# Attention over 1,426 keys: the last 32 keys' scores once per image, the last pair's sum on TensorE, third expert layers every other step

## The chip, the cores and the metric

One core of one Trainium2 chip runs the whole network in one launch. The metric is the device time of that launch in microseconds. Before the change three runs took 3327.84 to 3328.48 us, median 3328.4. The profiled execution has a span of 3332.1 us; all shares below are of that span.

## The reference, cut to what matters

The input is 8 images of 256 channels and 32 x 32 places, float32. Layer 0 is an attention with pooled keys, layer 1 an attention over 1024 tokens and then eight experts. The change touches the softmax attention of layer 0 and the end of the experts:

```python
# layer 0, for each image: 8 heads of 32 channels, 1024 queries, N = 1024 + 256 + 121 + 25 = 1426 keys
attn = softmax(einsum('bhqd,bhkd->bhqk', q_g, k) * SCALE, axis=-1)
out_att = einsum('bhqk,bhkd->bhqd', attn, v)
# layer 1, experts: three layers per expert e, weighted by a gate per place
h = relu(bn(einsum('bfd,edh->bfeh', x, W1)))
h = relu(bn(einsum('bfeh,ehk->bfek', h, W2)))
y = einsum('bfeh,ehd->bfed', h, Wo) + bo
out = einsum('bfed,fe->bfd', y, w)
```

## The kernel before, in words

**Recording layer.** Nearly every instruction goes through one helper (`call` in `Flow.Engine`, line 669), so the profile shows line 669 for all of them and names have to be told by their tiles. `Flow` also plans: it keeps a modelled clock for each engine (`cost`, `now`), and background work is written as generators ("threads"). Between two pieces of the main loop `f.step(pace)` runs threads whose inputs are ready by the model, with a credit of TensorE time given by `PACE` (threads of high rank) and `PACE1` (those of rank 5 and above). `f.finish(cond)` runs threads until a condition holds. All this happens when the program is built. On the chip the order on each engine is then fixed, and only semaphores remain.

**The attention stage, 0 to about 2,000 us.** A unit is one image `b`, one half `c` of the heads (four heads) and one half of the queries (512), so there are 4 units per image and 32 in all. `KEY_CHUNKS` (line 43) cuts the 1,426 keys into 12 chunks: eleven of 128 and a last one of 18. The main loop has a step for each unit and chunk, 384 steps:

- `scores`: four matmuls, one for each head, each 32 rows of the array, write the tile `sc` [128 keys, 4 heads, 512 queries]. `sc` is four PSUM banks, and there is only one of it. ScalarE then writes exp of it into a tile `pt` (1 MB; there are six buffers).
- `values` of the step before: four matmuls, one for each head, each 32 columns of the array, add up in `pv` over the 12 chunks.
- After each odd chunk, `add` issues a DMA from GpSimd's queue that adds this `pt` to the one before it in place (`accum_op`), so a pair becomes one tile.
- `sums`, a thread of rank 0 for each unit: VectorE adds pair after pair to the first (five pairs, two instructions each), then TensorE multiplies the total with ones (four matmuls of 32 columns) and so sums over the 128 keys. ScalarE copies the result into `rec`, and `normalise` divides.

As background run the pooled maps, convolutions and layernorms of the next image's keys and values, and layer 1's attention for the image before.

**The expert stage, about 2,000 to 3,332 us.** There are 128 items (16 tiles of 512 places, eight experts). `first7` and `second` compute layers one and two by seven block products each (tile `bank`), which VectorE combines (`sums`). `second(i, True)` writes its result to DRAM, and `fetch` reads it back. `weigh` multiplies it by the gate on VectorE and makes the combinations `t` for the third layer, on VectorE or GpSimd. `third` does seven products into `y`. Third layers can't start before the gate is known, which needs the mean over all images; by then the second layers are 24 or so ahead. The loop at the end of `experts` (from line 2339) lets the third layers catch up: while `many` is true, it does two of them in each iteration. For the first of the two, GpSimd makes the combinations and, for the second, VectorE.

Of the kernel before, what the change touches and what calls it, by code (L numbers as in the profile page):

```python
# [16 lines left out]
P = 128  # L17
C = 256
HW = 1024
HEADS = 8  # L20
DH = 32
# [7 lines left out]
FILLER = 5  # L29
PACE = 4.0  # L30
PACE1 = 2.0
CAP = (1.5, 1.5)
# [9 lines left out]
LIMIT = 1e12  # L42
KEY_CHUNKS = [(i * P, min(P, NK - i * P)) for i in range(NKC)]
KEY_SLICES = [(0, 512), (512, 512), (1024, 402)]
# [98 lines left out]
def layer0_general(tc, kit, nb, x, t1, consts, consts8, vecs, q_t, kv_t, proj_t, gqk_t):  # L143
    nc = tc.nc
    T = kit.tile
    with ExitStack() as ctx:
# [189 lines left out]
        def transpose_values(b):  # L336
            acc = vs.pop(b)
            for i in range(0, NKC, 2):
                ps = T(psum, [P, 512], "sm")
                part = KEY_CHUNKS[i : i + 2]  # L340
                for u, (k0, w) in enumerate(part):
                    for c in range(2):
                        o = u * C + c * P
                        nc.tensor.transpose(ps[:w, o : o + P], acc[:, c, k0 : k0 + w], ident)
                whole = [part] if part[-1][1] == P else [part[:1], part[1:]]
                u = 0
                for group in whole:
                    w, g = group[0][1], len(group)
                    src = ps[:w, u * C : (u + g) * C].rearrange("p (a j d) -> p a j d", j=2, d=DH)
                    dst = vext[:w, i + u : i + u + g].rearrange("p u a s d -> p (u a) s d")  # L350
                    nc.vector.tensor_copy(dst[:, :, 0, :], src[:, :, 0, :])
                    nc.scalar.copy(dst[:, :, 2, :], src[:, :, 1, :])
                    u += g

        def global_token(b):
# [21 lines left out]
            ps = T(psum, [P, 512], "sm")  # L377
            for kc, (k0, w) in enumerate(KEY_CHUNKS):
                nc.tensor.transpose(ps[:w, kc * 8 : kc * 8 + 8], pg[:, k0 : k0 + w], ident[:HEADS, :HEADS])
            pt = T(work, [P, NKC * 8], "gpt")  # L380
            last, lw = (NKC - 1) * 8, KEY_CHUNKS[-1][1]
            nc.vector.tensor_copy(pt[:, :last], ps[:, :last])
# [3 lines left out]
            ps = T(psum, [P, 512], "sm")  # L386
            for kc, (k0, w) in enumerate(KEY_CHUNKS):
                nc.tensor.matmul(
                    ps[:HEADS, :C],
                    lhsT=pt[:w, kc * 8 : kc * 8 + 8],  # L390
                    rhs=vext[:w, kc, :, 0::2, :],
                    start=kc == 0,
                    stop=kc == NKC - 1,
                )
# [144 lines left out]
        def attend(n, background, steps):  # L539
# [4 lines left out]
            for half in range(2):  # L544
# [13 lines left out]

                for kc, (k0, w) in enumerate(KEY_CHUNKS):
                    t = T(psum, [P, 2, 512], "sc")  # L560
# [95 lines left out]
class Flow:  # L656
# [54 lines left out]
    def cost(self, engine, op, out, ins):  # L711
# [9 lines left out]
        if engine == "PE":  # L721
            if op == "transpose":
                return 0.13
            c = max(0.2, 0.00169 * n)
            return c if self.tiling(ins) is None else c / 4
        psum = any(i.space == PSUM for i in ins)
# [153 lines left out]

def attention(tc, kit, f, outer, ended, nb, consts, x, t1, t2, hn, bounds, vecs, q_t, kv_t, proj_t, gqk_t, wqk, wqkv, vecs1, w1_d, w1c, gate_d, wrc, vecs2, bnvec):

# [5 lines left out]
    with ExitStack() as ctx:  # L888
# [160 lines left out]

        ks, qs, vts = {}, {}, {}  # L1050
        made = [0]
        turn = [-1]
# [199 lines left out]
        def by_tokens(accs, dst, k0):  # L1252
# [4 lines left out]
            for i in range(0, 4, 2):  # L1257
                span = slice(chunks[i][0], sum(chunks[i + 1]))
                yield pe(*(acc[:, span] for acc in accs), tag="sm")
                ps = small()  # L1260
                for u, (o0, w) in enumerate(chunks[i : i + 2]):
                    for c in range(2):
                        o = u * C + c * P
                        f.pe.transpose(ps[:w, o : o + P], accs[c][:, o0 : o0 + w], ident)
                w = chunks[i + 1][1]
                if w == P:
                    f.act.activation(dst[:, i : i + 2, :], ps.rearrange("p (u c) -> p u c", u=2), AF.Copy)
                else:
                    f.act.activation(dst[:, i, :], ps[:, :C], AF.Copy)
                    f.act.activation(dst[:w, i + 1, :], ps[:w, C:], AF.Copy)  # L1270
            yield ve(dst)
# [155 lines left out]
        def key_tokens(b, g):  # L1427
# [7 lines left out]
            for c in range(2):  # L1435
# [5 lines left out]
                ps = small()  # L1441
                for u, (_, tw) in enumerate(KEY_CHUNKS[4 * g : 4 * g + 4]):
                    f.pe.transpose(ps[:, u * P : u * P + tw], kt[:tw, u, c * P : (c + 1) * P], ident[:tw, :tw])
                f.act.activation(ks[b, c][:, s0 : s0 + w], ps[:, :w], AF.Copy)
# [18 lines left out]
        def scores(b, c, sl, kc):  # L1463
# [7 lines left out]
            return pt  # L1471

        def values(b, c, kc, pt, pv):
            w = KEY_CHUNKS[kc][1]
# [17 lines left out]
        def sums(n, pairs):  # L1492

            for i in range(1, NKC // 2):
                yield until(lambda: len(pairs) > i)
                for j in range(0, 4, 2):
                    s = pairs[0][:, j : j + 2, :]
                    yield ve(s, pairs[i])
                    f.ve.tensor_tensor(s, s, pairs[i][:, j : j + 2, :], ALU.add)
            yield until(lambda: normalised[0] == n)  # L1500
            yield pe(pairs[0], tag="sm")
            total = small()
            for j in range(4):
                f.pe.matmul(
                    total[DH * j : DH * j + DH, :], lhsT=kit.ones[:, :DH], rhs=pairs[0][:, j, :], start=True, stop=True
                )
            rec = T(work, [P, 512], "rec")
# [303 lines left out]
        f.spawn(layer1(), 6)  # L1811
        steps = [(b, c, half, kc) for b in range(nb) for c in range(2) for half in range(2) for kc in range(NKC)]

        pts = {}
        for i in range(len(steps) + 1):
            if i < len(steps):
                b, c, half, kc = steps[i]
                sl = slice(half * 512, half * 512 + 512)
# [8 lines left out]
                if b == 0 and kc == 0:  # L1827
                    f.finish(lambda: (c, half) in asked)
                pts[i] = scores(b, c, sl, kc)
                f.step()  # L1830
            if i:
                b1, c1, half1, kc1 = steps[i - 1]
                if kc1 == 0:
                    pv = T(psum, [P, 512], "pv")
                    pairs = []
                    sl1 = slice(half1 * 512, half1 * 512 + 512)
                    f.spawn(unit(b1, c1, sl1, i // NKC, pairs), 0)
                f.finish(lambda: kc1 // 4 in vts[b1])
                values(b1, c1, kc1, pts[i - 1], pv)
                if kc1 % 2:  # L1840
                    add(kc1, pts.pop(i - 1), pts[i - 2])
                    pairs.append(pts.pop(i - 2))
                if kc1 == NKC - 1:
# [145 lines left out]
def experts(tc, kit, nb, t2, hn, h2d, w1c, w2_d, wo_d, bnvec, bo_d, gate_d, wrc, consts8, gtd, out, f, outer, ended, early):  # L1989
# [12 lines left out]
    with ExitStack() as ctx:  # L2002
# [336 lines left out]
        while n3 < total:  # L2339
            many = n2 > n3 + 2  # L2340
            if n2 < n1 - 1 or n1 == total and n2 < total:
                second(n2, many)
                n2 += 1
                if many:
                    weighed(f.pool)
                    thirds()
            weighed(f.ve if many else f.pool)
            if n1 < total:
# [6 lines left out]
def tile_conv_attn_hybrid(  # L2355
# [45 lines left out]
    with ExitStack() as early:  # L2401
# [5 lines left out]
        attention(  # L2407
            tc, kit, f, (l1, shared), ended, nb,
            consts, x, t1, t2, hn, bounds, vecs0, q_t, kv_t, proj_t, gqk_t, wqk, wqkv, vecs1, w1_d, w1c, gate_d, wrc, vecs2, bnvec,
# [124 lines left out]
```

## Time and profile before

| engine | busy, us | share | what it does in the attention step |
|---|---|---|---|
| TensorE (PE) | 3137.4 | 94% | scores, values, ones-products, background |
| its weight loads (PEld) | 1912.8 | 57% | overlap with the matmuls |
| VectorE (DVE) | 2472.4 | 74% | pair sums, convolutions, normalisation |
| ScalarE (ACT) | 1734.4 | 52% | exp, evacuation of PSUM |
| GpSimd (POOL) | 1227.3 | 37% | issues the accumulating DMAs; layer combinations in the experts |

A matmul in float32 stands as two records, so the counts of TensorE records are about twice those of instructions. Groups of the attention step that matter for the change:

| group | records | mean of one, us |
|---|---|---|
| exp, `pt<-sc` | 384 | 1.875 |
| pair sums on VectorE, `pt<-pt,pt` | 320 | 1.254 |
| scores, `sc<-q,kn` | 3072 | 0.650, four at a time |
| values, `pv<-pt,vt` | 3072 | 0.620, four at a time |
| accumulating DMA of 1024 KB, `pt<-pt` | 160 | 7.4 from issue to landing |
| the same of 144 KB (18 keys) | 32 | 4.5 from issue to landing |

The page gives busy time, then what made the engine wait. Busy time of one engine lies beside that of others. Work taken away from an engine counts only where another one waited for it. A wait is written as "who <- for whom: us in total, times, longest".

### The profile page before, as it was taken

The page shows a single profiled execution, that of the slowest core. Times are in us where ns is not written, and L with a number is a line of the kernel's source. Part 1 is how long each engine was busy: PE and PEld are TensorE (multiplying, and loading weights), DVE is VectorE, ACT ScalarE, POOL GpSimd, SP SyncE. Part 2 cuts the span into 40 slices and gives each one's busy share as a digit, 9 for nine tenths or more (in the row PEclk, how much of TensorE's full clock was granted, in tenths as well). Part 3 has the DMA queues.
Part 4 walks back from the last instruction along what each step waited for, and adds up shares of the span by engine and source line. Part 5 has one row for each costly group of instructions (what it writes and reads, how often), then busy time and mean ns, then how long its engine had stood idle before and what let it go on. Part 6 is the DMA issues. An engine that isn't in the chain of part 4 may idle for free.

```text
span 3332.1 us, 42942 instructions
## 1 busy us (share of the span) xinstructions
PE 3137.4 (94%) x15970; PEld 1912.8 (57%) x15970; DVE 2472.4 (74%) x4069; ACT 1734.4 (52%) x2328; POOL 1227.3 (37%) x1300
## 2 busy tenths in 40 slices
PE   8687899999999999899899999999999999999997
PEld 4332244344344344344345346777888888888886
DVE  5687788786887886886884555446998787787776
ACT  4476676666576566576566543333233444444442
POOL 2211413213213214213211112006666776777775
PEclk9798999999999999999999999999999999999999
DMA  2357656656646646656556656124442010000000
GB/s 74 82 121 158 131 106 146 133 101 154 133 100 157 135 104 147 135 120 123 121 125 133 133 119 237 70 88 159 158 146 102 20 45 26 20 20 32 20 13 21
DMA packets 106666, 347.10 MB, mean 104 GB/s; under 512 B 13056, under 2 KB 38408, under 8 KB 83216
## 3 DMA queue, kind: packets, MB, share of 16 engines
q0 software_dynamic: 28608, 179.85, 28.1%
q1 hardware_dynamic: 74480, 162.45, 14.1%
q8 instruction: 128, 2.10, 0.3%
q10 hardware_dynamic: 3360, 1.97, 0.2%
q14 instruction: 90, 0.74, 0.1%
HBM read 105.11 MB, written 73.97 MB: 54 GB/s over the span
## 4 chain that ended last, share of the span: by engine, by line
PE 57%; DVE 5%; issue 3%; ACT 3%; POOL 3%; DMA 2%; SPq 0%; DVEq 0%; POOLq 0%; ACTq 0%
PE bank L669 18%; PE sm L669 13%; PE y L669 8%; PE sc L669 6%; PE sx L669 6%; PE pv L669 5%; DVE h L669 2%; ACT pt L669 2%; POOL tm L669 1%; DVE u L669 1%; DMA pt<-pt 1%; ACT h L669 1%; POOL t L669 1%; DVE t L669 1%; DVE c L669 1%
## 5 line engine op out<-in xcount | busy, mean ns | idle before, releaser
L669 ACT ACTIVATE pt<-sc 128x2048 f32<-128x2048 f32 (+1 forms) x384 | 719.9, 1875 | 326.5 <-PE sc L669 272.7
L669 DVE SCALAR_TENSOR_TENSOR acc<-p,vec,acc 128x225 f32<-128x225 f32 (+7 forms) x928 | 526.6, 574 | 29.3 <-ACT acc L669 4.8
L669 PE MATMUL sc<-q,kn 32*128 32x512 f32 (+1 forms) x3072 | 445.6, 650 | 94.7 <-ACT pt L669 92.9
L669 DVE TENSOR_TENSOR pt<-pt,pt 128x1024 f32<-128x1024 f32 x320 | 387.4, 1254 | 144.3 <-DMA pt<-pt 135.3
L669 POOL DMA_DIRECT2D pt<-pt x192 | 174.0, 907 | 780.1 <-ACT pt L669 615.7
L669 PE MATMUL pv<-pt,vt 128*32 128x512 f32 (+1 forms) x3072 | 420.6, 620 | 0.0
L669 ACT ACTIVATE p1c<-bank 128x256 f32<-128x256 f32 x228 | 87.2, 383 | 576.4 <-PE bank L669 576.1
L669 ACT ACTIVATE h<-h,bnvec 128x512 f32<-128x512 f32 x456 | 345.0, 805 | 50.7 <-DVE h L669 43.7
L669 POOL TENSOR_TENSOR rstd<-rstd,mhalf 128x4 f32<-128x4 f32 (+2 forms) x88 | 107.0, 1216 | 673.8 <-DVE rstd L669 635.0
L669 DVE TENSOR_TENSOR h<-p1c,bank 128x512 f32<-128x512 f32 x228 | 155.2, 681 | 194.7 <-PE bank L669 191.2
L669 PEld LDWEIGHTS sc<-q,kn 32*128 32x128 f32 (+1 forms) x3072 | 116.1, 178 | 285.8 <-ACT pt L669 184.9
L669 POOL TENSOR_TENSOR tm<-h,tm 128x256 f32<-128x256 f32 x206 | 247.6, 1202 | 16.1
L669 DVE TENSOR_TENSOR h<-u,bank 128x256 f32<-128x256 f32 x456 | 232.1, 550 | 7.9
L669 PEld LDWEIGHTS pv<-pt,vt 128*32 128x32 f32 (+1 forms) x3072 | 60.7, 108 | 301.7 <-issue 290.3
L669 POOL TENSOR_TENSOR tm<-h 128x512 f32<-128x512 f32 x103 | 133.9, 1300 | 245.2 <-ACT h L669 241.2
L669 DVE TENSOR_TENSOR h<-h,gate 128x1024 f32<-128x1024 f32 x128 | 209.1, 1642 | 2.5 <-DMA h<-h 2.1
L669 PE MATMUL bank<-h,w2e 128*128 128x256 f32 (+1 forms) x612 | 198.8, 453 | 4.1 <-DVE h L669 4.1
L669 PE MATMUL y<-t,s3e 128*128 128x256 f32 x768 | 188.0, 381 | 10.6 <-POOL t L669 10.3
L669 POOL TENSOR_TENSOR t<-h,t 128x256 f32<-128x256 f32 x210 | 177.4, 845 | 16.5
L669 PE MATMUL bank<-t,s1e 128*128 128x256 f32 x750 | 182.3, 379 | 0.0
L669 PE MATMUL sm<-y,t 128*128 128x256 f32 x752 | 180.6, 385 | 0.0
L669 DVE TENSOR_TENSOR u<-h,bank 128x512 f32<-128x512 f32 x228 | 156.7, 687 | 24.0
(316 smaller groups left out, 5604.3 us busy)
## 6 DMA issues: line engine op xcount, KB each, us to landing
pt<-pt POOLq DMA_DIRECT2D x160, 1024.0 KB, 7.4
h<-h SPq DMA_DIRECT2D x90, 512.0 KB, 3.2
xi<-in_x_dram SPq DMA_DIRECT2D x16, 512.0 KB, 6.7
t<-t SPq DMA_DIRECT2D x8, 1024.0 KB, 9.7
res<-t SPq DMA_DIRECT2D x32, 256.0 KB, 3.9
t<-res SPq DMA_DIRECT2D x32, 256.0 KB, 5.4
hn<-res SPq DMA_DIRECT2D x32, 256.0 KB, 3.0
hn<-hn SPq DMA_DIRECT2D x16, 512.0 KB, 4.2
```

The source lines that it names most:

```text
L669: ins = fn(*args, **kwargs)
```

## The change

**The last 32 keys.** `KEY_CHUNKS` now cuts ten chunks of 128, one of 114 and one of 32 (`LAST`). The scores of the last chunk are computed once per image, for all four units: `last_scores` places unit `n` on the score tile's partitions 32n to 32n + 31, by 16 matmuls of 32 x 32, and one exp serves all four. The part of unit 0 is used in place. Those of units 1 to 3 are written to small DRAM tiles (`lasts`), and `fetch_last` reads each back to partitions 0 to 31 of a `pt` tile, two steps before its unit ends. An image has 12 + 3 x 11 = 45 steps instead of 48. In units 1 to 3 the values of chunks 10 and 11 follow each other in one step.

**The last pair.** `sums` leaves the last pair (chunks 10 and 11) out of VectorE's additions. It gets four ones-products of its own, which accumulate onto those of the first tile. The tile of the last pair is so kept until then.

**Pace.** The credits per step are raised from 4.0 and 2.0 to 4.3 and 2.15, since the same background has to fit in fewer steps.

**Third layers.** In the loop of the experts the additional third layer comes only with every other second layer, with its combinations on VectorE; the regular one has them on GpSimd. The catching up takes about twice as many iterations.

```diff
-PACE = 4.0
-PACE1 = 2.0
+PACE = 4.3
+PACE1 = 2.15
...
+LAST = 32
+KEY_CHUNKS = [(i * P, P) for i in range(NKC - 2)]
+KEY_CHUNKS += [((NKC - 2) * P, NK - LAST - (NKC - 2) * P), (NK - LAST, LAST)]
...
+            if self.key(out).startswith("sc") and ins[0].shape[-1] == LAST:
+                return c / 16
...
+        def last_scores(b):
+            k0 = KEY_CHUNKS[-1][0]
+            t = T(psum, [P, 4, 512], "sc")
+            for n in range(4):
+                c, half = divmod(n, 2)
+                for j in range(4):
+                    r = slice(DH * j, DH * j + DH)
+                    f.pe.matmul(
+                        t[LAST * n : LAST * n + LAST, j, :],
+                        lhsT=ks[b, c][r, k0:],
+                        rhs=qs[b, c][r, half * 512 : half * 512 + 512],
+                        start=True,
+                        stop=True,
+                    )
+            pt = T(work, [P, 4, 512], "pt", bufs=6)
+            f.act.activation(pt, t, AF.Exp, scale=SCALE0)
+            for n in range(1, 4):
+                f.sp.dma_start(lasts[n - 1], pt[LAST * n : LAST * n + LAST])
+            return pt
+
+        def fetch_last(n):
+            pt = T(work, [P, 4, 512], "pt", bufs=6)
+            f.sp.dma_start(pt[:LAST], lasts[n - 1])
+            return pt
...
-            for i in range(1, NKC // 2):
+            last = NKC // 2 - 1
+            for i in range(1, last):
...
-            yield until(lambda: normalised[0] == n)
-            yield pe(pairs[0], tag="sm")
+            yield until(lambda: len(pairs) > last and normalised[0] == n)
+            yield pe(pairs[0], pairs[last], tag="sm")
             total = small()
-            for j in range(4):
-                f.pe.matmul(
-                    total[DH * j : DH * j + DH, :], lhsT=kit.ones[:, :DH], rhs=pairs[0][:, j, :], start=True, stop=True
-                )
+            w = KEY_CHUNKS[2 * last][1]
+            for p, k in ((pairs[0], P), (pairs[last], w)):
+                for j in range(4):
+                    f.pe.matmul(
+                        total[DH * j : DH * j + DH, :],
+                        lhsT=kit.ones[:k, :DH],
+                        rhs=p[:k, j, :],
+                        start=k == P,
+                        stop=k == w,
+                    )
...
+        steps = [
+            (b, n, kc) for b in range(nb) for n in range(4) for kc in range(NKC if n == 0 else NKC - 1)
+        ]
...
-                pts[i] = scores(b, c, sl, kc)
+                if kc == NKC - 1:
+                    f.finish(lambda: (b, 1) in qs and (b or len(asked) == 4))
+                    pts[n, kc] = last_scores(b)
+                else:
+                    pts[n, kc] = scores(b, c, sl, kc)
+                if n and kc == NKC - 3:
+                    pts[n, NKC - 1] = fetch_last(n)
...
-                values(b1, c1, kc1, pts[i - 1], pv)
-                if kc1 % 2:
-                    add(kc1, pts.pop(i - 1), pts[i - 2])
-                    pairs.append(pts.pop(i - 2))
+                for kc1 in (kc1, NKC - 1) if n1 and kc1 == NKC - 2 else (kc1,):
+                    f.finish(lambda: kc1 // 4 in vts[b1])
+                    values(b1, c1, kc1, pts[n1, kc1], pv)
+                    if kc1 % 2:
+                        add(kc1, pts.pop((n1, kc1)), pts[n1, kc1 - 1])
+                        pairs.append(pts.pop((n1, kc1 - 1)))
...
-                if many:
-                    weighed(f.pool)
+                if many and n2 % 2:
+                    weighed(f.ve)
                     thirds()
-            weighed(f.ve if many else f.pool)
+            weighed(f.pool)
```

## The prediction

> **What bounds the kernel now.** I read the page's head first: busy shares, then the tenths over time.
>
> ```profile
> PE 3137.4 (94%) x15970; PEld 1912.8 (57%) x15970; DVE 2472.4 (74%) x4069; ACT 1734.4 (52%) x2328; POOL 1227.3 (37%) x1300
> ...
> PE   8687899999999999899899999999999999999997
> ...
> DVE  5687788786887886886884555446998787787776
> ACT  4476676666576566576566543333233444444442
> ```
>
> TensorE is at nine tenths or more nearly from slice 5 on. So the time is TensorE's work plus its idle time, 3332 - 3137 = 195 us; the other engines matter where they make TensorE wait. Next, the busy time by stage: one stretch of attention, three of the expert stage.
>
> ```profile
> core 0: us, PE busy (x) PEld busy (x) DVE busy (x) ACT busy (x) POOL busy (x), PEclk, DMA share, GB/s
> 1000.00:1250.00 250.00, 241.94 (x1381) 113.80 (x1379) 204.35 (x372) 162.34 (x200) 61.30 (x74) 1.00 0.60 132
> 2300.00:2500.00 200.00, 189.91 (x867) 163.18 (x865) 183.58 (x229) 58.29 (x97) 138.63 (x133) 1.00 0.42 146
> 2500.00:2700.00 200.00, 196.69 (x905) 171.26 (x904) 165.49 (x227) 75.14 (x123) 135.50 (x122) 1.00 0.16 58
> 2700.00:2900.00 200.00, 199.27 (x921) 174.47 (x920) 157.53 (x223) 82.59 (x135) 143.31 (x132) 1.00 0.09 30
> ```
>
> Attention: TensorE 97%, VectorE 82%, ScalarE 65%. Experts: 921 matmul records per 200 us once the third layers have caught up (0.217 us each), but 867 and 905 while they catch up. Last, what TensorE waits for, and the groups of the attention step.
>
> ```profile
> PE sc L669 <- ACT pt L669: 92.9, 92, 3.6
> PE y L669 <- POOL t L669: 10.3, 9, 1.8
> ```
>
> ```profile
> L669 ACT ACTIVATE pt<-sc 128x2048 f32<-128x2048 f32 (+1 forms) x384 | 719.9, 1875 | 326.5 <-PE sc L669 272.7
> ...
> L669 DVE TENSOR_TENSOR pt<-pt,pt 128x1024 f32<-128x1024 f32 x320 | 387.4, 1254 | 144.3 <-DMA pt<-pt 135.3
> ```
>
> ```profile
> 778.74 1.14 PE L669 MATMUL sc<-q,kn 32*128 32x512 f32 x8
> 779.81 1.06 PE L669 MATMUL pv<-pt,vt 128*32 128x512 f32 x8
> 780.81 1.99 PE L669 MATMUL sx<-p,v 128*128 128x256 f32 x8
> ```
>
> The second view is one step on TensorE: scores (1.07 us to the next start), values (1.00), background. The next scores start at 782.73, so the step is 3.99 us; less 8 records at 0.217 it costs 2.25 us besides its background. A step without background is 1.07 + 1.88 (exp) + 0.19 = 3.14 us, of which TensorE idles 1.0: it needs the exp out of the single score buffer. These idle microseconds are most of the 92.9.
>
> **What the skill says.** "TensorEngine Tiling (Array Packing)", Key Properties: a change of tiling mode drains TensorE, and tiles run independently. The trace agrees: values take 1.00 us up to a change of mode, but 0.88 where a ones-product of the same mode follows (25 times). "TensorE: Matmul & The Clock Gate", Part 3: four row tiles (K = 32, N = 512) ran 3.07 times as fast as one by one, sixteen (K = M = 32) 10.6 times. No matmul here uses sixteen. The same page, Part 1: ScalarE's queue is strictly in order; the exp that waits for a buffer holds back all ScalarE work behind it, and the trace never shows another.
>
> **Part 1: scores of the last 32 keys once per image.** Steps go from 384 to 360. ScalarE loses 24 exps x 1.875 = 45 us, beside TensorE. TensorE: a removed step costs 2.25 us, but its values stay and follow those of the chunk before in the same mode, 0.88. Saved: 24 x 1.37 = 32.9 us. The eight shared score groups have 16 tiles. Low price, from the skill's ratios: (16/10.6)/(4/3.07) x 1.07 = 1.24 us, or 0.2 us more each, 1.6 in all. High: the four column tiles of a row strip run one after another, 4 x 1.07 = 4.3, 26 us in all. I take 1.6, because values, with four column tiles and four different streams, already overlap. The 24 writes and 24 reads of 256 KB go on SyncE's queue: 3.0 us (hn<-res) and 3.9 to 5.1 (res<-t, gate<-gtd) to land. The writes have some nine steps until the first read; a read is issued two steps before its values. Time for them: 6.3 us at least, so nothing, if the read's buffer is free.
>
> **Part 2: ones-products.** VectorE loses 64 adds x 1.254 = 80 us, beside TensorE. TensorE gains 32 groups x 0.88 = 28.2 us on the path. So TensorE's work changes by -32.9 + 28.2 + 1.6 = -3 us: a wash.
>
> **Background per step (PACE).** Background does not change in amount. I priced what stands between values and next scores in the built programs' order (0.84 us per pass of 512 columns and so on). Before: 65 steps have none, 51 less than 1 us, and the shortfalls below 1 us sum to 82.6 (measured wait: 92.9). After: 62 and 42 of 360, sum 76.6. Gain: 6 x 92.9/82.6 = 7 us. About 24 us of layer-1 work of the last image moves behind the attention stage, where TensorE is busy anyway: no change.
>
> **The new wait: six pt buffers.** Before, a unit keeps one (the running sum) to its end. Now it keeps two, and the fetched chunk takes one as well. In the built order the exps that overwrite a source of an accumulating DMA come closer to it: issued one exp earlier 0 -> 6 times, two 16 -> 66, three 154 -> 92. The DMA lands a median 8.3 us after its exp ends (issue 0.9, 7.4 to landing). With short steps the exp has 3 x 3.14 - 1.88 = 7.5 us at distance two (0.8 late), and 2 x 3.14 - 1.88 = 4.4 at one (3.9 late). Queued behind: all ScalarE work, then the next scores. Going through the order with these numbers, 16 exps come late after and one before; leaving out steps whose background covers it, 12 us against 0.6. The measured 17.5 us ("ACT pt <- DMA pt<-pt") shows that slow landings add to such counts. Low: 0. High: 40 us, that is all 22 us of the late ones plus as much again from slow landings. I take +10.
>
> **Part 3: third layers every other step.** While catching up, one iteration holds first, second and two thirds: 56 records x 0.217 = 12.2 us; VectorE has about 4.8 (two sums) + 3.3 (two gate products, 1.64 each) + 2.2 (one combination) = 10.3 of it, and GpSimd's combination is used in the same iteration: "PE y <- POOL t". Now two iterations hold seven layers, 21.3 us, and VectorE about 17. The deficit against 921 records is 54 + 16 = 70 records, 15 us. I take -11 (bounds 0 and -15). The catch-up lasts from about the 23rd to the 64th second layer instead of the 45th: 19 more round trips of 512 KB, at a DMA share of 0.16 or less, hidden.
>
> **Sum.** -3 - 7 + 10 - 11 = -11: 3328.4 - 11 = 3317.
>
> **Rivals.**
> - *More is gained*: VectorE and ScalarE at 82% and 65% give way, background is ready earlier and the exps that start late by ScalarE's backlog (20 steps, 30.6 us of TensorE idle) shrink by a third; buffers cost nothing. For it: a wait for DVE or ACT stands ahead of many background pieces. Against: TensorE idles 3% only. -3 - 7 - 10 - 15 = -35: 3293.
> - *The buffers become the bound; slower*: +40 from late exps and fetches, and sixteen tiles at half the high price, +12, so -3 + 12 - 7 + 40 - 11 = +31: 3359; with cheap tiles 3347. For it: the DMA distances, and TensorE's clock, which halved after a 2.5 us wait at 670 us (scores 1.67 instead of 1.14). Against: long steps hide most of them.
> - *A wash*: the buffers take all that the expert stage gives, +20 - 3 - 7 - 11 = -1: 3327.
>
> **Numbers.** Forecast 0.47, more gained 0.17, wash 0.18, slower 0.18. The forecast's own spread puts a few hundredths into no change, and the wash's a few into either side: faster 0.60, same 0.19, slower 0.21. Range 3290 to 3346: it takes in the larger gain and the slower case with cheap tiles.
>
> **What the profile after would show.** Exps 360, VectorE adds 256; score groups with 16 tiles near 1.2 us (4.3: the high price is right). "PE sc <- ACT pt" near 90 us in total if gaps and buffers balance; above 115 the slower rival is right, below 75 the larger gain. "ACT pt <- DMA pt<-pt" above 17.5. The window 2300:2500 above 900 records, "PE y <- POOL t" near 2 us. Wrong if TensorE's records in attention lengthen, or if values of the fetched chunk wait for their read.

## The result, and the profile after

| | us, median | smallest to largest |
|---|---|---|
| before | 3328.4 | 3327.8 to 3333.5 (4 runs) |
| after | 3348.4 | 3340.2 to 3352.7 (4 runs) |

The ratio is 1.0054, with a 95% interval of 1.0032 to 1.0075: the change costs about 18 us. The forecast was 3317, a gain, and the time lies just above its range. The profiled executions differ by less, 3332.1 against 3345.9 us from first to last instruction: in the device's own time the one of before took 3334.6 us, 6.2 above its median, and the one of after 3347.7, 0.7 below. The accounts below are of these two executions, 13.8 us apart, so they explain somewhat less than the measured loss.

From the page of the kernel after, first the head and the tenths of TensorE, then three groups of the attention step: records, busy time and mean in ns of one, then the idle time ahead of them and what ended most of it.

```profile
PE 3137.9 (94%) x16226; PEld 1922.1 (57%) x16226; DVE 2383.8 (71%) x4002; ACT 1693.4 (51%) x2304; POOL 1206.6 (36%) x1303
...
PE   8687899999999889899999889999999999999997
...
L672 ACT ACTIVATE pt<-sc 128x2048 f32<-128x2048 f32 (+1 forms) x360 | 675.7, 1877 | 290.2 <-PE sc L672 220.3
...
L672 PE MATMUL pv<-pt,vt 128*32 128x512 f32 (+2 forms) x3072 | 420.1, 621 | 12.0 <-DMA pt<-last 12.0
...
L672 DVE TENSOR_TENSOR pt<-pt,pt 128x1024 f32<-128x1024 f32 x256 | 312.9, 1264 | 116.5 <-DMA pt<-pt 116.2
```

The work moved as intended: 24 exps and 64 additions fewer, VectorE 89 us and ScalarE 41 us less busy. TensorE is as busy as before (3137.9 against 3137.4), so the loss is idle time: 208.0 us instead of 194.7. The tenths show five eights from slice 14 to 24, in the later half of the attention stage and at its end, where there were two. The line of the values shows the first new thing: they wait 12.0 us for the read of the last chunk.

TensorE's idle time by stage, summed from the gaps in the trace:

| stage | before, us | after, us |
|---|---|---|
| up to the first scores | 14.8 | 13.5 |
| attention, first to last scores | 133.1 | 154.4 |
| last scores to the first third layer | 12.3 | 11.7 |
| first third layer to TensorE's last instruction | 19.8 | 13.8 |
| the rest, nearly all after that | 14.7 | 14.6 |

The wait tables (who <- for whom: us in total, times, longest) of TensorE and of ScalarE after, and of ScalarE before:

```profile
PE sc L672 <- ACT pt L672: 105.0, 81, 5.4
PE pv L672 <- DMA pt<-last: 12.0, 2, 9.4
...
PE y L672 <- POOL t L672: 2.3, 3, 1.3
```

```profile
ACT pt L672 <- DMA pt<-pt: 54.6, 20, 6.8
```

```profile
ACT pt L669 <- DMA pt<-pt: 17.5, 9, 3.2
```

Fewer waits of the scores for the exp (81, not 92) cost more (105.0, not 92.9): the longest is 5.4 us instead of 3.6. The exps' own wait says why. They wait 20 times instead of 9 for an accumulating DMA that still reads or writes the `pt` buffer they are to overwrite, three times as long in all. Going through the 20 and the 9 in the trace, the gaps of the next scores sum to 37 us after and 17 before.

One such wait in three views of the kernel after: GpSimd's timeline, ScalarE's and TensorE's (start, duration, in brackets the idle time ahead and its releaser).

```profile
1633.29 1.04 POOL L672 TENSOR_TENSOR rstd<-rstd,mhalf 128x4 f32<-128x4 f32 x1 [8.00 <-DVE rstd L672]
1634.30 0.90 POOL L672 DMA_DIRECT2D pt<-pt  x1
```

```profile
1636.69 1.88 ACT L672 ACTIVATE pt<-sc 128x2048 f32<-128x2048 f32 x1 [1.26 <-PE sc L672]
...
1644.18 1.88 ACT L672 ACTIVATE pt<-sc 114x2048 f32<-114x2048 f32 x1 [4.65 <-DMA pt<-pt]
```

```profile
1639.67 1.07 PE L672 MATMUL pv<-pt,vt 128*32 128x512 f32 x8
1646.11 2.09 PE L672 MATMUL sc<-q,kn 32*128 32x512 f32 x8 [5.37 <-ACT pt L672]
1648.13 3.79 PE L672 MATMUL pv<-pt,vt 114*32 114x512 f32 x16
```

The exp of chunk 7 ended at 1631.4, but its accumulating DMA stood behind `rstd` in GpSimd's queue and was issued 2.9 us later, at 1634.30; `rstd` itself had waited for VectorE (GpSimd was idle for 8.00 us ahead of it). It landed at 1644.08. The exp of chunk 10 (114 keys), with two exps between, waits for it and starts at 1644.18, 5.6 us after the end of the exp before it. TensorE's next scores wait 5.37 us. They then take 2.09 us instead of 1.13, and the values of two chunks behind them 3.79: the granted clock is at half from 1644.2 to 1657.9. This late buffer is paid twice, as a gap and as slow work after it. The fetch of this unit's last chunk, issued at 1635.96, holds one of the six buffers meanwhile.

The longest wait for a read, on SyncE's queue and on TensorE:

```profile
1215.10 0.60 SPq L672 DMA_DIRECT2D t<-in_x_dram  x1
1215.75 0.72 SPq L672 DMA_DIRECT2D res<-t  x1
1216.69 0.46 SPq L672 DMA_DIRECT2D pt<-last  x1
```

```profile
1221.45 1.06 PE L672 MATMUL pv<-pt,vt 114*32 114x512 f32 x8
1231.89 1.93 PE L672 MATMUL pv<-pt,vt 32*32 32x512 f32 x8 [9.38 <-DMA pt<-last]
```

The 256 KB read was issued 5.8 us ahead of its values' turn, but landed 15.2 us after its issue, behind a 1 MB transfer issued 1.6 us before it on the same queue, which landed at 1230.2. From 1221 to 1227 us an accumulating DMA moved 0.99 MB on GpSimd's queue; SyncE's queue moved 0.55 MB in these 6 us, after 1.91 MB in the 7 us before. The median of the 17 reads whose landing the trace gives is 4.4 us.

How much of TensorE's busy time is lost to the clock can be worked out: its busy time within the stretches below full clock, times the share of the clock that is missing.

| us | busy | lost to the clock | difference |
|---|---|---|---|
| before | 3137.4 | 46.3 | 3091.1 |
| after | 3137.9 | 49.9 | 3088.0 |

So the work fell by 3.1 us, as small as forecast, and slow clock took 3.6 back.

The expert stage, in the windows of the prediction (columns as there):

```profile
2300.00:2500.00 200.00, 196.49 (x897) 169.44 (x896) 159.86 (x222) 67.43 (x112) 147.83 (x167) 1.00 0.42 149
2500.00:2700.00 200.00, 197.23 (x911) 172.49 (x910) 163.93 (x228) 70.49 (x117) 119.35 (x112) 1.00 0.41 145
2700.00:2900.00 200.00, 198.36 (x915) 173.17 (x914) 160.22 (x227) 76.91 (x127) 133.43 (x125) 1.00 0.19 64
```

Against 921 records per 200 us the deficit is 24 + 10 + 6 = 40 records, 9 us at 0.217, instead of 70 records. The windows hold slightly later work here, since the first third layer starts at 2301 us instead of 2280: TensorE's busy time between the first expert products and that layer grew from 273.7 to 296.3 us, as the forecast had it (24 us of layer-1 work of the last image left the attention stage and now stands behind it). The round trips rise from 90 to 130 and are hidden.

### The profile page after: what moved, and what is told of

Read it like the earlier page. It is cut to its first block, busy times and chain, and to the rows that moved or that the text cites. A ratio compares the mean times of both kernels' runs of the same rounds, so it can differ in the third digit from the quotient of the medians.

```text
span 3345.9 us, 43540 instructions
## 1 busy us (share of the span) xinstructions
PE 3137.9 (94%) x16226; PEld 1922.1 (57%) x16226; DVE 2383.8 (71%) x4002; ACT 1693.4 (51%) x2304; POOL 1206.6 (36%) x1303
## 3 DMA queue, kind: packets, MB, share of 16 engines
q10 hardware_dynamic: 3360, 1.97, 0.2%
## 4 chain that ended last, share of the span: by engine, by line
PE 70%; DVE 5%; DMA 5%; ACT 3%; issue 2%; POOL 2%; SPq 0%; DVEq 0%; ACTq 0%; POOLq 0%
PE bank L672 20%; PE sm L672 18%; PE y L672 10%; PE sc L672 8%; PE sx L672 8%; PE pv L672 7%; DMA pt<-pt 3%; ACT pt L672 2%; DVE h L672 1%; DVE u L672 1%; DVE c L672 1%; DVE acc L672 1%; DMA pt<-last 1%; DVE rec L672 1%; DMA feat<-hn 0%
## 5 line engine op out<-in xcount | busy, mean ns | idle before, releaser
L672 ACT ACTIVATE pt<-sc 128x2048 f32<-128x2048 f32 (+1 forms) x360 | 675.7, 1877 | 290.2 <-PE sc L672 220.3
L672 PE MATMUL sc<-q,kn 32*128 32x512 f32 (+2 forms) x3072 | 423.0, 653 | 105.8 <-ACT pt L672 105.0
L672 PE MATMUL pv<-pt,vt 128*32 128x512 f32 (+2 forms) x3072 | 420.1, 621 | 12.0 <-DMA pt<-last 12.0
L672 DVE TENSOR_TENSOR pt<-pt,pt 128x1024 f32<-128x1024 f32 x256 | 312.9, 1264 | 116.5 <-DMA pt<-pt 116.2
L672 PEld LDWEIGHTS sc<-q,kn 32*128 32x128 f32 (+2 forms) x3072 | 113.9, 179 | 292.0 <-ACT pt L672 190.7
L672 POOL TENSOR_TENSOR tm<-h,tm 128x256 f32<-128x256 f32 x206 | 238.8, 1159 | 16.1
L672 PEld LDWEIGHTS pv<-pt,vt 128*32 128x32 f32 (+2 forms) x3072 | 61.1, 109 | 317.0 <-issue 292.5
L672 DVE TENSOR_TENSOR h<-h,gate 128x1024 f32<-128x1024 f32 x128 | 200.5, 1566 | 0.5 <-ACT h L672 0.5
L672 DVE RECIPROCAL rec<-rec 128x512 f32<-128x512 f32 x32 | 107.3, 3352 | 108.2 <-ACT rec L672 108.2
L672 POOL TENSOR_TENSOR t<-h 128x512 f32<-128x512 f32 x106 | 137.5, 1298 | 106.8 <-DVE h L672 83.9
```

What stands on the lines that cost most here:

```text
L672: ins = fn(*args, **kwargs)
```

## The experiments

Every ratio is to the kernel before, run beside it on the same chip; times of different groups are compared by their ratios. Three explanations were open. The **buffers** (six `pt` tiles are too few, and the fetch comes late), the **order** (another pace gives another planned order, lucky or not), and **VectorE** (its relief, which the prediction costed at nothing).

### Which part costs

Part 3 alone, on the kernel before (e1):

```diff
-                if many:
-                    weighed(f.pool)
+                if many and n2 % 2:
+                    weighed(f.ve)
                     thirds()
-            weighed(f.ve if many else f.pool)
+            weighed(f.pool)
```

> The kernel before with the experts' loop of the change alone (additional third layer every other step). Theory (attention stage lost about 21 us of TensorE idle, the experts gave about 6): 6 to 8 us faster than before, near 3321, with 2300:2500 near 897 records instead of 867. Rival (the loop's longer catch-up with its 20 more round trips to DRAM is what costs): 5 us or more slower than before.

The kernel after, with this edit reversed (e2):

> The changed kernel with the experts' loop as before. Theory: the whole loss lies in the attention stage, so 6 to 8 us slower than the changed kernel: near 3355, 0.8% above before. Rival (loss in the experts): back to within 5 us of before.

Part 2 alone, on the kernel before (e4):

```diff
-            for i in range(1, NKC // 2):
+            last = NKC // 2 - 1
+            for i in range(1, last):
...
-            yield until(lambda: normalised[0] == n)
-            yield pe(pairs[0], tag="sm")
+            yield until(lambda: len(pairs) > last and normalised[0] == n)
+            yield pe(pairs[0], pairs[last], tag="sm")
...
+            for p in (pairs[0], pairs[last]):
+                for j in range(4):
+                    f.pe.matmul(
...
+                        start=p is pairs[0],
+                        stop=p is pairs[last],
```

> The kernel before with the last pair summed by ones-products of its own, and nothing else of the change. Work alone: TensorE +28 us, so 3328 + 28 = 3356 if VectorE's relief of 80 us buys nothing. Theory A (a kept tile costs buffer waits): above that, 3360 to 3370, with the exps' wait for the accumulating DMA above 30 us instead of 17.5. Rival (VectorE's relief brings background earlier): below 3345.

The kernel after with part 2 undone (e3): VectorE adds the last pair again, on its 114 keys, and the ones-products run on the total alone.

```diff
-            last = NKC // 2 - 1
-            for i in range(1, last):
+            for i in range(1, NKC // 2):
                 yield until(lambda: len(pairs) > i)
+                w = KEY_CHUNKS[2 * i][1]
...
-            for p, k in ((pairs[0], P), (pairs[last], w)):
-                for j in range(4):
...
+            for j in range(4):
```

> The changed kernel with the last pair added by VectorE again, so that its tile is free after the add and four ones-products are enough; last scores per image and thirds stay. Theory A (the pt buffers are the cause, and the kept tile is a part of it): TensorE loses 32 x 0.88 = 28 us of work, VectorE gains 77 us, exps wait less for accumulating DMAs (54.6 us falls towards 30): 3310 to 3325. Rival B (only the fetch through DRAM holds the buffer and costs; the kept tile costs nothing): faster by the 28 us of work alone with the wait for DMA still above 50 us, near 3320. Rival C (VectorE is needed): its adds delay background, no faster than 3340.

| parts of the change | us | ratio to before | 95% interval |
|---|---|---|---|
| 3 alone | 3319.7 | 0.9971 | 0.9960 to 0.9982 |
| 2 alone | 3338.8 | 1.0036 | 1.0022 to 1.0049 |
| 1 and 2 | 3353.3 | 1.0079 | 1.0066 to 1.0093 |
| 1 and 3 | 3362.6 | 1.0109 | 1.0092 to 1.0127 |
| 1, 2 and 3 | 3348.4 | 1.0054 | 1.0032 to 1.0075 |

Part 1 stands here with the raised credits. Part 3 does what was forecast: 0.0029 x 3328 = 9.7 us by itself, 0.0025 or 8 us in the changed kernel. "PE y <- POOL t" falls from 10.3 to 2.0 us. Of all kernels here that compute everything it is the fastest, faster than both before and after.

Part 1 is what costs: 1 and 3 lose 43 to 46 us against 3 alone, although TensorE's busy time falls from 3134.7 to 3124.5. The wait tables of the kernel with parts 1 and 3, ScalarE's and TensorE's:

```profile
ACT pt L672 <- DMA pt<-pt: 49.2, 17, 6.8
...
ACT pt L672 <- DVE pt L672: 22.8, 10, 4.0
```

```profile
PE sc L672 <- ACT pt L672: 110.5, 97, 5.3
```

The expectations had this kernel between 3310 and 3325 by the buffers or by the fetch alone, and at 3340 or more if VectorE matters. It came out at 3363, so the first two missed. Without the kept tile the exps wait about as long for DMAs (49.2 us), and 22.8 us for VectorE's additions to free a tile (4.8 in the kernel after). Doing without the kept tile gains no buffer here, then: the pair waits for VectorE instead. The planned order differs too.

Part 2 alone adds 26.8 us of TensorE work (3137.4 to 3164.2; 28.2 was priced), but takes 13.9 us of idle time away (194.7 to 180.8, of which 6.3 in attention) and costs 10 to 12 us. The buffer theory had 3360 to 3370 here and missed, although the exps' wait for DMAs rose to 28.6 us. On top of parts 1 and 3 part 2 gains 14 to 18. So it was not worth nothing to take 80 us from VectorE, or else the ones-products themselves fill gaps in which TensorE would have waited for an exp; no run separates the two.

### A seventh buffer

A seventh `pt` tile needs 8 KB per partition more than there is. Room was made by dropping the values of the keys from 1024 on, for which those of the second group of keys are used. This omission also changes the planned order, so each kernel with seven has its own control with six. The seventh buffer alone does not: in the traces of each such pair all engines have the same instructions in the same order, so the two differ in the buffers only.

```diff
+            if g == 2:
+                yield until(lambda: 1 in vts[b])
+                vts[b][2] = vts[b][1]
+                return
-            vt = T(work, [P, 4, C], "vt", bufs=6)
+            vt = T(work, [P, 4, C], "vt", bufs=4)
...
-            pt = T(work, [P, 4, 512], "pt", bufs=6)
+            pt = T(work, [P, 4, 512], "pt", bufs=7)
```

The kernel after with this omission, six (e5) and seven buffers (e6):

> Left out: the token-major values of keys 1024 and up are not made; the values of keys 512 to 1023 stand in for them, so that four vt buffers are enough and 8 KB per partition come free. Otherwise the changed kernel, with six pt buffers: the control of the next. Expected of all theories: a little background less (8 transposes, a few copies per image), some 5 to 15 us below the changed kernel, with the exps' wait for the accumulating DMA still near 50 us.

> The same as the control (the same values left out), with seven pt buffers in the room that came free. Theory A (the sixth buffer is what the change lacks): the exps' wait for the accumulating DMA falls from some 50 us below 15, TensorE's idle time in attention by 20 us or more, the time by 15 to 35 us against the control. Rival B (the trip of the last chunk through DRAM or its place in the order costs, not the buffers): within 6 us of the control.

The kernel before with it, six (e9) and seven (e10):

> The kernel before with the same values left out as in e5 (token-major values of keys 1024 and up), six pt buffers: the control of the next. 5 to 25 us less than before by the work left out.

> The same with seven pt buffers. Theory A (six were enough before, and the change needs one more): within 8 us of its control, against the 20 us that the seventh buffer gave in the changed kernel. Rival (the kernel before was short of buffers just as much): 15 us or more faster than its control.

| with the omission | six: us, ratio | seven: us, ratio | gain |
|---|---|---|---|
| after | 3324.5, 0.9982 (0.9976 to 0.9989) | 3304.3, 0.9918 (0.9902 to 0.9933) | 20 to 21 us |
| before | 3333.9, 1.0008 (0.9998 to 1.0018) | 3324.5, 0.9985 (0.9977 to 0.9992) | 8 to 9 us |

ScalarE's and TensorE's waits in the kernel after with the omission, first with six buffers, then with seven:

```profile
ACT pt L672 <- DMA pt<-pt: 56.9, 19, 6.8
```

```profile
PE sc L672 <- ACT pt L672: 101.3, 82, 5.5
```

```profile
ACT pt L672 <- DMA pt<-pt: 18.8, 9, 4.1
```

```profile
PE sc L672 <- ACT pt L672: 87.4, 87, 3.9
```

One buffer brings the wait back to what it is before the change (17.5, 9 times), and "PE sc <- ACT pt" from 101.3 to 87.4. TensorE's idle time in attention falls from 140.8 to 124.4, and its busy time by 3.2, which is less slow clock. The time is as expected; the wait (below 15) and the idle time (20 less) fell a little short of it. The kernel before gains less than half as much, about the 8 us that were allowed it. With seven buffers and the same omission the changed kernel is 0.9985 - 0.9918 = 0.0067 faster, 22 us, of which part 3 has 8 to 10: the change is a good one where the buffers suffice.

The controls say something too. The omission takes about 7 us of TensorE's work from the kernel after (3088.0 to 3081.0 without the clock) and 8 from the kernel before (to 3083.1). The kernel before gains nothing by it (5 to 25 us were expected), but the kernel after gains 24 us (5 to 15 were expected), with the exps' wait for DMAs as long as ever (56.9 us). So in this other order the change gains 9 us (0.9982 against 1.0008) with six buffers. That total wait is not the loss, and the loss of 18 us belongs to the change's own order as well as to its buffers.

The opposite, one buffer less in the kernel before with nothing left out (e18; again the same instructions in the same order):

```diff
-            pt = T(work, [P, 4, 512], "pt", bufs=6)
+            pt = T(work, [P, 4, 512], "pt", bufs=5)
```

> The kernel before with five pt buffers instead of six. Theory A (a buffer held longer is like a buffer less): 15 us or more slower, with the exps' wait for the accumulating DMA above 40 us instead of 17.5. Rival (the order covers it): within 8 us.

```profile
ACT pt L669 <- DMA pt<-pt: 117.6, 40, 8.6
```

3387.6 us, ratio 1.0175 (1.0158 to 1.0191): 58 us slower with the same work. TensorE is busy 3158.3 us instead of 3137.4, of which 67.1 instead of 46.3 are lost to the clock: the difference is 3091.2, the same work to 0.1 us. The profiled execution is 48.9 us longer than that of before: 20.8 of it are slow clock after gaps, 28.0 idle time. From five to six the kernel before gains 58 us, from six to seven (with the omission) 8 to 9, so six stood near the knee of its curve; the changed kernel, which gains 20 by the seventh, stands on the steeper side.

### The fetch

No fetch (e7): units 1 to 3 do without the last 32 keys' values and sums. With it go 24 groups of values and 24 of the accumulating DMAs.

```diff
-            for n in range(1, 4):
-                f.sp.dma_start(lasts[n - 1], pt[LAST * n : LAST * n + LAST])
...
-                if n and kc == NKC - 3:
-                    pts[n, NKC - 1] = fetch_last(n)
...
-                for kc1 in (kc1, NKC - 1) if n1 and kc1 == NKC - 2 else (kc1,):
+                for kc1 in (kc1,):
...
```

> Left out: in units 1 to 3 the last 32 keys are neither written to DRAM nor fetched, and have no values and no part in the sums; the shared scores and their exp stay. TensorE loses 24 x 0.88 = 21 us of work. Theory A (a pt buffer taken at chunk 9, and the wait for the read): 21 + 12 (wait for the read) + 10 to 20 of late exps less than the changed kernel: 3295 to 3305. Rival (the fetch costs nothing beside its work): 3348 - 21 - 12 = 3315 at best, with the exps' wait for the DMA still at 50.

3293.6 us, ratio 0.9885 (0.9867 to 0.9904), 56 us less than the kernel after by the ratios. 21 us of it are busy time, mostly matmuls left out (busy 3116.8); that leaves 35 us for having the fetch (30.3 of idle time in the profiles), of which 12 are the wait for the read. ScalarE's wait for DMAs falls to 24.8 us. The buffer theory had 3295 to 3305, its rival 3315 at best. As the planned order differs too, the 35 us are not the fetch's alone for certain.

The fetch one step later (e12), so that it holds its buffer for a shorter time:

```diff
-                if n and kc == NKC - 3:
+                if n and kc == NKC - 2:
                     pts[n, NKC - 1] = fetch_last(n)
```

> The changed kernel with the fetch of the last chunk issued with the scores of chunk 10 instead of chunk 9, so that it takes its pt buffer one step later. Theory A: fewer late exps at chunk 10 (the exps' wait for the DMA falls by 10 to 20 us), but the read, 4.4 us, has one step only: TensorE's wait for it rises from 12 to 20 to 50 us; 3335 to 3360. Rival (the hold of the buffer costs nothing): the wait for the read comes on top, 3355 or more.

```profile
PE pv L672 <- DMA pt<-last: 41.1, 12, 6.5
```

3383.9 us, ratio 1.0157 (1.0141 to 1.0173). The reads now come too late 12 times, as expected, and TensorE is busy 3157.6 us, of which 69.3 are lost to the clock (3088.3 without it, the work of the kernel after). The time was expected between 3335 and 3360, or at 3355 or more if the buffer's hold costs nothing; and the exps' wait for DMAs was expected to fall, but rose to 70.6 us. This edit also gives another planned order (TensorE's differs from 808 us on), so the run shows that one step is not enough room for the read, and not what the shorter hold is worth.

### The order

The pace alone, in the kernel after (4.3 and 2.15 as changed): 4.0 (e8), 4.2 (e16), 4.6 (e15), and in the kernel before (4.0 and 2.0): 4.3 (e11), 3.7 (e17). `PACE1` is half of it each time. The edit of e8; the others differ from it in the two numbers alone:

```diff
-PACE = 4.3
-PACE1 = 2.15
+PACE = 4.0
+PACE1 = 2.0
```

> The changed kernel with the credits of before, 4.0 and 2.0 instead of 4.3 and 2.15. Theory A (buffers): within 8 us of the changed kernel either way, 3340 to 3356. Rival C (the higher credits burn the background early in a unit and leave bare steps, in which late exps are felt): 10 us or more faster than the changed kernel.

> The changed kernel with credits 4.2 and 2.1, between those of e8 and of the change. Theory A: above before, 3335 to 3375. Rival (unlucky order): at or below before. If the credit itself counts and not the order, it lies between the changed kernel (3348) and e8 (3374).

> The changed kernel with credits 4.6 and 2.3. Theory A (six buffers cost in any order, the order only says how much): above before in every order, 3335 to 3375. Rival (the order of the change was an unlucky one): at or below before, 3328.

> The kernel before with the credits of the change, 4.3 and 2.15. Theory A' (with 45 steps for the same background the higher credit is needed, with 48 it isn't): within 8 us of before. Rival (the higher credit is worth 25 us in any of these kernels, as between the changed kernel and e8): 15 us or more faster than before.

> The kernel before with credits 3.7 and 1.85. If the kernel before has slack in its buffers, the order matters little: within 10 us of before. If it moves by 20 us or more, the order alone explains as much as the change lost.

| credit | 3.7 | 4.0 | 4.2 | 4.3 | 4.6 |
|---|---|---|---|---|---|
| before: ratio | 1.0007 | 1 | | 1.0002 | |
| after: ratio | | 1.0128 | 1.0025 | 1.0054 | 0.9997 |
| after: "ACT pt <- DMA pt<-pt", us | | 76.7 | 48.4 | 54.6 | 38.1 |

The kernel before hardly reacts to its credits, although its order changes with them. The kernel after moves by 0.0131, 44 us, and its time rises with the exps' wait for DMAs through all four. So the order is a cause too. That it works through the buffers, and decides which exps come late where they are short, fits the wait but is not shown: the changed kernel with seven buffers was not run at other credits, and with the omission another order removed the loss without removing the wait. The buffer theory had the kernel above before in every order (3335 to 3375); it missed at 4.6, where the loss is gone (0.9988 to 1.0006), and its 3340 to 3356 for 4.0 missed as well. Yet even at 4.6 the kernel stays behind part 3 alone, 0.9971. The four orders tried lose 0.0026 to 0.0157 against that.

### VectorE, with buffers

To take the buffers out of the question for part 2, the kernel of parts 1 and 3 was given the omission, with six (e13) and with seven buffers (e14):

> The kernel of e3 (last pair added by VectorE) with the values left out as in e5, six pt buffers: the control of the next. Slower than e5 (0.998 of before) if VectorE's add is what makes e3 slow: 1.004 to 1.010 of before.

> The same with seven pt buffers. Theory A (six buffers are the cause in e3 as well): 25 us or more faster than its control and, as TensorE has 28 us less work than in e6, at or below 3300. Rival (VectorE holds back TensorE there): still above 3315.

3338.3 us, 1.0028 (1.0018 to 1.0039) and 3320.9 us, 0.9976 (0.9969 to 0.9984). The buffer is worth 17 us here too, though 25 or more were expected, and the control came out a little faster than expected (1.004 to 1.010). With seven the exps hardly wait for DMAs (14.8 us), TensorE does 24 us less than with the ones-products (3102.1 against 3126.1), and the kernel is still 0.0058, 19 us, slower. TensorE's wait table with seven buffers, first of this kernel, then of the one with the ones-products (e6):

```profile
PE sc L672 <- ACT pt L672: 102.0, 93, 7.5
PE sm L672 <- ACT kt L672: 11.2, 24, 1.5
```

```profile
PE sc L672 <- ACT pt L672: 87.4, 87, 3.9
...
PE sm L672 <- ACT kt L672: 5.8, 12, 1.5
```

The idle time in attention is 162.7 against 124.4: where VectorE (73% busy) has the additions, TensorE waits 38 us more. The two other pairs of changed kernels that differ in this point agree (180.0 against 154.4, and 172.6 against 140.8 with six buffers and the omission). The waits that a result of VectorE itself ends differ by 5 us only (19.3 against 14.0), those that ScalarE ends by 36. Which of VectorE's results come late, whether a better order would hide them, and how much of this is gaps filled by the ones-products, was not settled.

## Why the prediction was wrong, step by step

- **TensorE's work, -3.** The sum is right, -3.1 without the clock, but by errors that cancel. Part 3 alone has 1.3 of it (3134.7 - 44.9 = 3089.8), so the attention stage about -2. Part 1 saved 26 us, not 31 (parts 1 and 3 against part 3: 3063.7 against 3089.8), and part 2 on top cost 24, not 28 (3088.0). One reason stands in the trace: values were priced at 0.88 us where the fetched chunk's values follow, as in one mode, but those of 114 keys took 1.00 us to those of 32 keys, each of 19 times at full clock, as ahead of a change of mode. The 16-tile groups were cheaper than the low price: 1.07 to 1.09 us to the next group, eight times, as long as four tiles. What the step left out is the clock: +3.6.
- **Step gaps, -7.** Of the 105.0 us that scores wait for exps, 68 are not next to a late buffer, against 76 of 92.9 before: -8. That agrees, but does not confirm the step: the same sum is 60 to 79 us in the changed kernel at its four credits.
- **Six pt buffers, +10.** This step failed, in two terms. Late exps: the gaps next to them grew by 20 us (17 to 37), not 11. The counts of distances were right in direction, but the median landing (8.3 us after the exp) hid the late ones: the DMAs that held exps up landed 7.0 to 11.2 us after their issue, and 12 of the 20 were issued more than 1 us after their exp, up to 3.4 us. Second, the fetch was taken at "nothing, if the read's buffer is free". The reads landed in 2.9 to 15.2 us, and TensorE waited 12.0, 9.4 of it once. Together +32 where +10 was said, inside the bound of 40 that the slower rival used.
- **Third layers, -11.** Right: -9.7 alone, -8 in the changed kernel.
- **Work taken from VectorE, nothing.** Wrong in the kernel's favour: with it 14 us of idle time went in the kernel before (6 in attention), and 14 to 18 us of time, net, in the changed one. Whether VectorE's relief or gaps filled by the ones-products did this stays open.

Adding the measured terms as the profiles show them: idle in attention +21.3 (+20 late exps, -8 other gaps, +12 reads, -3 the rest), from the first third layer on -6.0, the other stages -2.0, TensorE's work -3.1 and its clock +3.6: +13.8 us.

The Trainium skill says in "TensorE: Matmul & The Clock Gate", Part 1, that the clock falls to half when the array has been idle and needs a few microseconds of work to come back. The traces agree: from 330 to 2,000 us the stretches at half clock last 3.41, 6.83, 10.24 or 13.65 us; there are 8 of them before (41.0 us) and 11 after (71.7 us). The prediction had seen one such wait and named it with the slower rival alone.

Of the rivals, the slower one named the mechanism and came within 2 us with cheap tiles (3347, for which 3348 was measured). That closeness is partly luck: its late exps and fetches were 40, not 32, it had no term for slow clock, and in the other three orders tried it would have been 10 to 24 us off. It was given too little chance, because the trace of before shows only nine late exps: but a resource that is not yet short says little when the change takes up to two of its six units.

What stays open: how much of the 28 us between part 3 alone and the kernel after belongs to this one order (at a credit of 4.6 only 9 us are left), and which of VectorE's results make TensorE wait. A seventh buffer without leaving anything out was not tried, for lack of room; nor was issuing the accumulating DMAs ahead of GpSimd's other work, which might make fewer exps late with six. Each profile is of one execution, so waits of a few microseconds carry little.

## What to carry to other kernels

When a change holds a buffer longer or adds a user of its pool, count who holds each one and until when, and compare with the landing times of the transfers that must end first, the late ones and not the median. A pool that shows few waits may still be at its knee: here the old kernel with one buffer less, 58 us slower, showed it. Measure the parts of a change by themselves; here, with six buffers, the part that stood beside the main idea carried all of the gain. And where a change moves a planned order, try a few orders before judging it: here they spread over 44 us.

## What the runs showed of the hardware that was not expected

- Sixteen tiles of 32 x 32 with 512 columns took 1.07 to 1.09 us to the next group, as four tiles of 32 rows do (1.07). The Trainium skill gives in "TensorE: Matmul & The Clock Gate", Part 3, ratios from which the prediction estimated 1.24.
- After a gap of 5.4 us, TensorE's clock stayed at half for 11.8 us of unbroken work. In the profile of the kernel with five buffers slow clock is 20.8 of the 48.9 us lost.
- An accumulating DMA onto 32 partitions (256 KB) took 4.6 us to land in the median, one onto 18 (144 KB) 4.5 and one onto 128 (1 MB) 7.4: a quarter of the data took 0.6 of the time.
- Values of 114 keys took 1.00 us to the values of 32 keys (19 times), as ahead of other work, and not the 0.88 us that values of 128 keys take where a ones-product of the same shape follows (24 times at full clock in the kernel before).
